# Two-layer transformer block on one core: projection copies on ScalarE, maxima ahead of layer 1, an earlier output load

## The chip, the cores and the metric

The kernel runs on one core of a Trainium2 chip. The metric is the device time in microseconds. A profile of one execution was taken besides; its times are in microseconds (us) unless a row says ns. Engines are named as in the profile: PE (TensorE matmul), PEld (its weight loads), DVE (VectorE), ACT (ScalarE), POOL (GpSimd) and SP (the queue that issues most DMAs).

## The reference

Two layers act on `x` of 4 x 512 x 320 (batch, tokens, channels); the context is 4 x 1601 x 192. There are 20 heads of 16 channels. Cut to what is computed, one layer is:

```python
h1 = _ln(x, n1_g, n1_b)
x = _attn(h1, h1, q1, k1, v1, o1_w, o1_b, heads) + x          # self-attention
h2 = _ln(x, n2_g, n2_b)
x = _attn(h2, context, q2, k2, v2, o2_w, o2_b, heads) + x     # cross-attention
h3 = _ln(x, n3_g, n3_b)
a, g = jnp.split(h3 @ ff_w1 + ff_b1, 2, axis=-1)              # 320 -> 2 x 1280
x = a * gelu(g) @ ff_w2 + ff_b2 + x                           # exact gelu, 1280 -> 320
```

and `_attn` projects q, k and v, takes softmax(q k^T / 4) v for each head, and multiplies the joined heads by `o_w`. All is float32.

## The kernel before

**Units.** The work of a layer is cut into 20 self-attention units, 20 cross-attention units and 4 feed-forward units, in this order. An attention unit is one batch element and one group of four heads; its keys (512, or 1601) are taken in chunks of 128. A feed-forward unit is one batch element. `u.i` is a unit's number in the whole order, `u.l` its layer, `u.kind` one of self, cross and ff.

**A chunk.** For each of four heads PE multiplies keys by queries into a PSUM bank `st` (128 keys x 512 queries; q and k are split into two parts for precision) and adds the negated row maximum through a product with ones (L1324). ACT raises each of the four to an exponential `pr` (L1334). PE then multiplies the chunk's `pr` with the values into one bank `av` (L1350); ACT copies that into `vo` (L1369), and POOL adds it to the unit's sum `o` (L1370). The values carry a column of ones, so the sum of the exponentials comes out beside them. The step from one `av` to the next is called a chunk below.

**What runs beside it.** The row maxima have to be known before a unit's scores: tiles `sps` of the scores of the unit ahead are made by PE (L1076, the last short key span L1101) and reduced by DVE (L1087, L1111) into `nmax` or `pm`. When all are there, L1155, L1158 and L1163 (`max_end`) negate, split and transpose them, and L1171 sends them by DMA to `nrows`. Between chunks PE also does the projections of later units: values `vps` (L1035), keys of the context `kps` (L972), queries `qps` (L947), queries and keys of self-attention `qkps` (L908), and the output projection `ops` (L1250).

**Copies out of PSUM.** The banks `vps` and `kps` are emptied by a copy that `taken` (L1011 to L1018) places: the recorded program keeps an estimate of when PE, DVE and ACT will be through with what they were given (`expect`), and the copy goes on DVE (L1014) where DVE's estimate is the earlier one, otherwise on ACT (L1017). `expect` also decides which of the eight PSUM banks a product gets: the one that comes free first. So a copy on another engine changes later choices of banks, and the places at which fillers are put.

**Order.** Everything is put in a fixed order when the program is recorded; the engines run their rows in that order. Small pieces of work sit in chains ("values", "proj", "divide" and others) with a due round, a round being one step of the record between groups of matmuls. After each chunk some are taken whose due rounds come and whose conditions hold. `giver` chooses, for a unit `u` that is running, the units ahead whose maxima tiles it may take beside its own work, and how many of them in each half chunk; for an attention unit these are the next two, for a feed-forward unit, before, the next one.

**Output.** When a batch element's heads are summed, `o` is written to memory (`oway`), read back in the layout of the output projection in three parts `aT` with the reciprocal sums `rT` (`load`, L1224 and L1225), POOL multiplies each part (`divide`, L1232), and PE projects (`project`, L1250). Each of these steps waits for a number of rounds after an earlier step: `since(i, n)` is n rounds after the i-th noted step. The third part's load follows its condition `since(4, 7)`, its multiply `since(5, 3)`, where the fifth note is made by that load.

**Feed-forward.** PE makes 320 to 2 x 1280 (L1435, L1495), ACT the gelu (L1506), DVE the product (L1507), PE the second product `yps` (L1542), and DVE adds it to `x` (L1549) for each of four blocks of 128 tokens.

Of the kernel before, what the change touches and what calls it, by code (L numbers as in the profile page):

```python
# [78 lines left out]
def kernel(ctx: ExitStack, tc: tile.TileContext, x, context, ws, out):  # L79
# [329 lines left out]
    expect = {"pe": 0.0, "act": 0.0, "dve": 0.0}  # L409
# [3 lines left out]
    def bank(name):  # L413
        i = min(range(NB), key=lambda i: bank_free[i])
        assert bank_free[i] < HELD, name
        t = psum.tile([P, 512], F32, tag=f"bank{i}", name=name)
        bank_of[id(t)] = [i, t, bank_free[i], 0.0]
        bank_free[i] = HELD
        return t
# [6 lines left out]
    def busy(engine, us, *tiles):  # L426
        expect[engine] = max([expect[engine]] + [bank_of[id(t)][3] + 0.05 for t in tiles]) + us
        for t in tiles:
            bank_free[bank_of[id(t)][0]] = expect[engine] + 0.09
# [12 lines left out]
    def add(chain, cost, f, due, ready=yes, soon=yes):  # L442
        chains[chain].append((cost if isinstance(cost, tuple) else (cost,), due, ready, soon, f))
# [566 lines left out]

    def taken(to, part, ps, us):  # L1011

        if expect["dve"] < expect["act"]:
            nc.vector.tensor_copy(to, part)  # L1014
            busy("dve", us, ps)
        else:
            nc.scalar.copy(to, part)  # L1017
            busy("act", us, ps)  # L1018
# [160 lines left out]
    def add_finish(u):  # L1179

        when = [clock["round"]]

        def since(i, n):
            return lambda: len(when) > i and clock["round"] >= when[i] + n

        def turn():

            way = o_way[u.b % 2]  # L1190
            dma(out=way[:, u.g * HG : (u.g + 1) * HG].rearrange("s j n -> j s n"), in_=u.o)
            if u.g == G - 1:
                held["written"] += 1
                errands.append((clock["round"] + 3, yes, sums))

        def sums():

            den = two.tile([P, N], F32, tag="rT", name="den")[:, : H * N // P]
            dma(out=den, in_=o_way[u.b % 2][DH].rearrange("h n -> (h n)").rearrange("(p c) -> p c", p=P))
            when.append(clock["round"])  # L1200

            def invert():
                nc.vector.reciprocal(den, den)
                busy("dve", 0.75)
                when.append(clock["round"])

            def save():
                dma(out=r_way[u.b % 2].rearrange("h n -> (h n)").rearrange("(p c) -> p c", p=P), in_=den)
                errands.append((clock["round"] + 3, lambda: held["open"] < 1, read))

            add("divide", LIGHT, invert, r - 20, yes, since(1, 3))
            add("divide", 0.0, save, r - 20, yes, since(2, 1))

        def read():

            held["read"] += 1
            held["open"] += 1
            aT = one.tile([P, 3, N], F32, tag="aT", name="aT")
            way, part = o_way[u.b % 2], {}

            def load(k, at, n):
                heads = slice(at // DH, (at + n) // DH)
                part[k] = two.tile([P, N], F32, tag="rT", name="rT")
                dma(out=aT[:n, k, :], in_=way[:DH, heads])  # L1224
                dma(  # L1225
                    out=part[k][:n],
                    in_=r_way[u.b % 2][heads].rearrange("(o j) n -> o j n", o=1).to_broadcast([DH, n // DH, N]),
                )
                when.append(clock["round"])

            def divide(k, n):
                nc.gpsimd.tensor_tensor(aT[:n, k, :], aT[:n, k, :], part[k][:n], ALU.mult)  # L1232

            for k, at, n in DK[:2]:
                load(k, at, n)
            first, second, third = DK
            add("divide", 0.0, lambda: divide(0, first[2]), r - 20, yes, since(4, 3))
            add("divide", 0.0, lambda: divide(1, second[2]), r - 20)
            add("divide", 0.0, lambda: load(*third), r - 20, yes, since(4, 7))
            add("divide", 0.0, lambda: divide(2, third[2]), r - 20, yes, since(5, 3))  # L1240
            add("divide", 0.0, lambda: end(aT), r - 20)

        def project(aT, t, part):
            cols = slice(part * D // 2, (part + 1) * D // 2)
            ps = bank("ops")
            written(0.93, ps)
            busy("dve", 0.3, ps)
            for k, at, n in DK:
                for f, m in tiles_of(P):
                    nc.tensor.matmul(  # L1250
                        ps[f : f + m, : D // 2],
                        lhsT=aT[:n, k, f * NQ + t * SLOT : f * NQ + t * SLOT + m],
                        rhs=wo[:n, k, cols],
                        start=(k == 0),
                        stop=(k == 2),
                    )
            nc.vector.tensor_tensor(xs[u.b][:, t, cols], ps[:, : D // 2], xs[u.b][:, t, cols], ALU.add)

        def end(aT):
            now = clock["round"]  # L1260
            for t in range(NQ):
                for part in range(2):
                    add(
                        "project", (0.317,) * 3, lambda t=t, part=part: project(aT, t, part),
                        now + 2 + u.nch * t + u.nch // 2 * part, yes, lambda: clock["round"] >= now + 1,
                    )
            add("project", 0.0, done, now + 2 + u.nch * NQ)

        def done():
            held["open"] -= 1  # L1270
            after(u)

        r = when[0]
        add("divide", 0.0, turn, r - 20, lambda: u.g or held["written"] < held["read"] + 2, since(0, 2))
# [327 lines left out]
    def left(v):  # L1602
        return sum(map(len, v.pairs))
# [19 lines left out]
    def giver(u):  # L1623

        ahead, coming = [], []
        for v in units[u.i + 1 : u.i + AHEAD + 1]:
            if v.kind == "ff":
                break  # L1630
            coming.append(v)
            if v.i <= u.i + 2 and (v.i == u.i + 1 or u.kind != "ff") or v.early:
                ahead.append(v)
                if v.pairs is None:
                    v.pairs = max_pairs(v)
        owed = 0.0
        last = clock["round"]

        def give(h, alone=False):
            nonlocal owed, last  # L1640
            rounds = []
            went = clock["round"] - last if alone else 1
            last = clock["round"]
            total = 0
            most = 0.0
            urgent = None
            for v in coming:
                if v not in ahead:
                    total += v.steps
                    continue  # L1650
                total += left(v)


                rest = v.start - (7 if alone else 4) - clock["round"]
                if rest > 0:
                    most = max(most, (total - rest * (not alone)) / (2 * rest))
                if left(v) and (rest == 1 or alone and rest < 1):
                    urgent = urgent or v
                    owed = max(owed, 1.0 if alone and rest > -4 else (left(v) + 1) // 2)
            owed += most * went if total else 0.0  # L1660
            while owed >= 1.0 and any(left(v) for v in ahead) and not (alone and rounds and rest > -4):
                hand = [v for v in ahead if left(v) and all(v.pairs) and at_hand(v)]
                if not hand and ahead[0].start - 4 - clock["round"] > 1:
                    break
                v = hand[0] if hand else next(v for v in ahead if left(v))
                if u.kind == "self" and ahead[-1].early and urgent is None:

                    v = ahead[-1]
                    if v not in hand:
                        break  # L1670
                at_once(v)
                rounds.append([f for q in v.pairs if q for f in q.popleft()[1]])
                owed -= 1.0
            owed = min(owed, 2.0)
            for v in ahead:
                mine = v.pairs[h % 2]
                if mine and not alone and at_hand(v):
                    return mine.popleft(), rounds
            return (False, []), rounds

        return give
# [46 lines left out]
    for i, u in enumerate(units):  # L1728
# [10 lines left out]
        for k in (3, SOON, AHEAD):  # L1739
            v = units[i + k] if i + k < len(units) else None  # L1740
# [32 lines left out]
```

## Time and profile before

| | |
|---|---|
| median of 3 runs | 2933.25 us (2932.35 to 2940.54) |
| profiled execution | 2933.88 us |
| its span, and mean granted clock | 2931.7 us, 0.994 |
| PE, DVE, ACT, POOL busy | 2863.0, 2069.9, 1881.4, 1299.4 us |
| copies of L1014 on DVE | 300 |
| copies of L1017 on ACT | 132 |

Layer 0's self-attention units run in about the first 290 us, its cross-attention units until about 1200, its feed-forward until 1505; layer 1 follows in the same order. In a row of the timeline the first number is the start from the span's beginning, the second the length of the row (a row may hold several instructions, xN), then engine, line, operation, output and inputs, and in brackets how long the engine was idle before it and what ended that. Busy shares of PE count a matmul that waits inside a run as busy, so PE's share does not tell how near it is to its limit; the length of chunks tells more.

### The profile page before, as it was taken

The numbers are of one execution on the slowest core, as the hardware profiler recorded it, in microseconds if no ns is written. First come the engines' busy times: TensorE is split into PE (matmuls) and PEld (weight loads), VectorE is DVE, ScalarE is ACT, GpSimd is POOL, SyncE is SP. The second block draws the span as 40 slices with busy tenths as digits, with TensorE's granted clock in tenths as the row PEclk, the third lists the DMA queues.
The fourth block names the chain that finished last, engine by engine and source line by source line (L and its number), as shares of the span: only waits on it lengthen the run. The fifth ranks groups of instructions, "written<-read, shape, count | busy, mean of one in ns | idle before, by whom it ended". The sixth has DMA issues, their size and how long they took to land.

```text
span 2931.7 us, 83446 instructions
## 1 busy us (share of the span) xinstructions
PE 2863.0 (98%) x35018; PEld 1540.3 (53%) x35018; DVE 2069.9 (71%) x4052; ACT 1881.4 (64%) x3733; POOL 1299.4 (44%) x1409
## 2 busy tenths in 40 slices
PE   8999999999999999999999999999999999999999
PEld 4445555555555555355554555555555555544554
DVE  6776888888888888323258678888888888872221
ACT  3767677887887888501138666778878778783000
POOL 3656345555545545211125663456455565551100
PEclk8999999999999999999999999999999999999999
DMA  3443223232232222200113342222221122222000
GB/s 106 113 120 99 68 73 101 59 85 62 49 93 61 54 54 62 84 17 11 42 38 88 99 104 69 58 62 53 62 65 47 50 72 51 53 56 76 22 20 14
DMA packets 163495, 188.59 MB, mean 64 GB/s; under 512 B 61988, under 2 KB 109104, under 8 KB 163120
## 3 DMA queue, kind: packets, MB, share of 16 engines
q1 hardware_dynamic: 162616, 181.69, 24.4%
q8 instruction: 275, 4.51, 0.6%
q10 hardware_dynamic: 472, 1.58, 0.2%
q14 instruction: 100, 0.82, 0.1%
q0 software_dynamic: 32, 0.00, 0.0%
HBM read 55.76 MB, written 29.36 MB: 29 GB/s over the span
## 4 chain that ended last, share of the span: by engine, by line
PE 87%; DVE 5%; POOL 2%; DMA 2%; ACT 2%; issue 1%; SPq 1%; ACTq 0%; POOLq 0%; DVEq 0%
PE av L1350 22%; PE st L1324 20%; PE fps L1435 10%; PE sps L1076 8%; PE yps L1542 6%; PE vps L1035 5%; PE kps L972 4%; PE ops L1250 4%; PE qkps L908 3%; PE fps L1495 3%; DVE nmax L1087 2%; PE qps L947 2%; DMA oway<-o 1%; PE sps L1101 1%; ACT pr L1334 1%
## 5 line engine op out<-in xcount | busy, mean ns | idle before, releaser
L1334 ACT ACTIVATE pr<-st 128x512 f32<-128x512 f32 (+1 forms) x2720 | 1404.5, 604 | 394.3 <-PE st L1324 359.3
L1087 DVE TENSOR_REDUCE pm<-sps 128x1 f32<-128x512 f32 (+1 forms) x1920 | 1147.8, 660 | 138.7 <-PE sps L1076 132.4
L1370 POOL TENSOR_TENSOR o<-o,vo 128x512 f32<-128x512 f32 x576 | 739.8, 1284 | 950.8 <-ACT vo L1369 942.0
L1076 PE MATMUL sps<-kT,q 32*128 32x512 f32 (+1 forms) x4800 | 869.0, 421 | 12.2 <-DMA q<-halves 4.4
L1324 PE MATMUL st<-q,kT 32*128 32x512 f32 (+1 forms) x5120 | 790.7, 420 | 2.8 <-ACT o L1364 2.4
L1350 PE MATMUL av<-pr,vals 128*32 128x512 f32 (+1 forms) x5440 | 734.5, 606 | 35.0 <-ACT pr L1334 13.4
L1324 PEld LDWEIGHTS st<-q,kT 32*128 32x128 f32 (+1 forms) x5120 | 448.5, 180 | 297.4 <-ACT pr L1334 117.5
L1324 PE MATMUL st<-nrows,ones 32*128 32x512 f32 (+1 forms) x2720 | 560.6, 399 | 4.8 <-DMA nrows<-turned 4.7
L1076 PEld LDWEIGHTS sps<-kT,q 32*128 32x128 f32 x4800 | 429.8, 184 | 73.7 <-DVE nmax L1087 14.6
L1087 DVE TENSOR_REDUCE nmax<-sps 128x1 f32<-128x512 f32 x640 | 396.7, 682 | 92.7 <-PE sps L1076 89.2
L1369 ACT COPY vo<-av 128x512 f32<-128x512 f32 x576 | 353.0, 613 | 17.4 <-PE av L1350 10.3
L1506 ACT ACTIVATE gl<-fps,b 128x512 f32<-128x512 f32 x80 | 54.7, 687 | 408.9 <-PE fps L1495 299.1
L1435 PE MATMUL fps<-hT,w 128*128 128x512 f32 x640 | 283.1, 597 | 0.0
L1350 PEld LDWEIGHTS av<-pr,vals 128*32 128x32 f32 (+1 forms) x5440 | 110.9, 108 | 309.9 <-DVE pm L1087 175.8
L1324 PEld LDWEIGHTS st<-nrows,ones 32*128 32x128 f32 (+1 forms) x2720 | 264.6, 180 | 14.8 <-DMA nrows<-turned 6.0
L1507 DVE SCALAR_TENSOR_TENSOR hid<-fps,b,gl 128x512 f32<-128x512 f32 x80 | 59.7, 748 | 242.6 <-ACT gl L1506 240.5
L1435 PEld LDWEIGHTS fps<-hT,w 128*128 128x128 f32 x640 | 119.2, 190 | 155.1 <-issue 152.2
L1542 PE MATMUL yps<-w,hid 128*128 128x320 f32 x640 | 175.5, 434 | 0.0
L1542 PEld LDWEIGHTS yps<-w,hid 128*128 128x128 f32 x640 | 120.6, 190 | 56.1 <-ACT gl L1506 5.3
L1250 PEld LDWEIGHTS ops<-wo,aT 112*32 112x32 f32 (+1 forms) x3072 | 99.3, 111 | 63.1 <-issue 29.5
L1250 PE MATMUL ops<-wo,aT 112*32 112x160 f32 (+1 forms) x3072 | 126.1, 302 | 5.5 <-POOL aT L1232 5.0
L527 POOL TENSOR_SCALAR root<-root 128x4 f32<-128x4 f32 x22 | 5.2, 234 | 266.8 <-DVE root L521 266.7
(91 smaller groups left out, 2544.1 us busy)
## 6 DMA issues: line engine op xcount, KB each, us to landing
kT<-stages SPq DMA_DIRECT2D x80, 400.5 KB
oway<-o SPq DMA_DIRECT2D x80, 256.0 KB
q<-halves SPq DMA_DIRECT2D x80, 256.0 KB
q<-halves SPq DMA_DIRECT2D x27, 512.0 KB
kT<-halves SPq DMA_DIRECT2D x40, 256.0 KB
aT<-oway SPq DMA_DIRECT2D x32, 224.0 KB
rT<-rway SPq DMA_DIRECT2D x32, 224.0 KB
hT<-hturned SPq DMA_DIRECT2D x96, 64.0 KB
```

The lines of the kernel that those rows point to most:

```text
L972: nc.tensor.matmul(ps[(i * GT + f) * SLOT : (i * GT + f + 1) * SLOT, :w], lhsT=wk2[:, k, u.g * GD + f * SLOT : u.g * GD + (f + 1) * SLOT], ...
L1035: nc.tensor.matmul(ps[f : f + m, :w], lhsT=u.kvT[:n, k, at + f : at + f + m], rhs=wv[:n, k, h0 * DH : h1 * DH], start=(k == 0), stop=(k == ...
L1076: nc.tensor.matmul(own[0][:, :w], lhsT=u.queries(slice(j * SLOT, (j + 1) * SLOT), e, t), rhs=u.kT[j * SLOT : (j + 1) * SLOT, u.k0 + at : u ...
L1087: nc.vector.tensor_reduce(to, own[0][:, :w], AX.X, ALU.max)
L1250: nc.tensor.matmul(ps[f : f + m, : D // 2], lhsT=aT[:n, k, f * NQ + t * SLOT : f * NQ + t * SLOT + m], rhs=wo[:n, k, cols], start=(k == 0) ...
L1324: nc.tensor.matmul(own[0][:r, :], lhsT=ones[rows, :r] if e == 2 else u.keys(rows, c), rhs=u.rows[rows, :] if e == 2 else u.queries(rows, e ...
L1334: nc.scalar.activation(p[:r], own[0][:r], AF.Exp)
L1350: nc.tensor.matmul(ps[j * SLOT : (j + 1) * SLOT, :], lhsT=columns_of[:r, head : head + SLOT], rhs=pr.pop((c, j))[:r, :], start=True, stop= ...
L1369: nc.scalar.copy(vo, ps)
L1370: nc.gpsimd.tensor_tensor(u.o, u.o, vo, ALU.add)
L1435: nc.tensor.matmul(ps, lhsT=w1[:, k, i * FF + c * P : i * FF + (c + 1) * P], rhs=natural(u.hT[:, k]), start=start, stop=stop,)
L1542: nc.tensor.matmul(ps[:, :D], lhsT=hid[c][:, t * P : (t + 1) * P], rhs=w2[:, c, :], start=(c == 0), stop=(c == NHC - 1),)
```

## The change

1. `taken` no longer compares: all copies of `vps` and `kps` are made by ACT (L1017).
2. `giver` lets a feed-forward unit take the maxima of the next two units as well. Only layer 0's last feed-forward has attention units right behind it, so this is the one place.
3. In layer 1 the third output load asks for five rounds after its mark, not seven.

```diff
     def taken(to, part, ps, us):
 
-        if expect["dve"] < expect["act"]:
+        if False:
             nc.vector.tensor_copy(to, part)
             busy("dve", us, ps)
         else:
...
-            add("divide", 0.0, lambda: load(*third), r - 20, yes, since(4, 7))
+            add("divide", 0.0, lambda: load(*third), r - 20, yes, since(4, 5 if u.l else 7))
             add("divide", 0.0, lambda: divide(2, third[2]), r - 20, yes, since(5, 3))
...
-            if v.i <= u.i + 2 and (v.i == u.i + 1 or u.kind != "ff") or v.early:
+            if v.i <= u.i + 2 or v.early:
                 ahead.append(v)
```

**DVE at the end of layer 0's last feed-forward.** `x_110` is the residual stream, `nmax_95` holds the maxima of layer 1's first unit and later those of its third, `nmax_96` those of the second. Before:

```order
L1549 TENSOR_TENSOR x_110<-yps,x_110 128x320
L1155 TENSOR_REDUCE nmax_95<-nmax_95 128x4x4
L1158 TENSOR_REDUCE nmax_95<-nmax_95 128x4x4
L1163 STREAM_TRANSPOSE turned<-nmax_95 128x32
L1549 TENSOR_TENSOR x_110<-yps,x_110 128x320
L1087 TENSOR_REDUCE nmax_96<-sps 128x1 x16
L1087 TENSOR_REDUCE nmax_95<-sps 128x1 x8
L1155 TENSOR_REDUCE nmax_96<-nmax_96 128x4x4
```

With the change:

```order
L1549 TENSOR_TENSOR x_110<-yps,x_110 128x320
L1087 TENSOR_REDUCE nmax_96<-sps 128x1 x4
L1155 TENSOR_REDUCE nmax_95<-nmax_95 128x4x4
L1158 TENSOR_REDUCE nmax_95<-nmax_95 128x4x4
L1163 STREAM_TRANSPOSE turned<-nmax_95 128x32
L1549 TENSOR_TENSOR x_110<-yps,x_110 128x320
L1087 TENSOR_REDUCE nmax_96<-sps 128x1 x12
L1087 TENSOR_REDUCE nmax_95<-sps 128x1 x4
L1155 TENSOR_REDUCE nmax_96<-nmax_96 128x4x4
```

Four reduces of the second unit went ahead of the first unit's `max_end`; between the last addition to `x` and the second unit's `max_end` there are 16 reduces, before 24.

**POOL in layer 1's self-attention,** at the output of the second batch element. Before:

```order
L1370 TENSOR_TENSOR o<-o,vo 128x512
L625 TENSOR_SCALAR hturned<-x_110,mv,root_25977 128x4x32
L625 TENSOR_SCALAR hturned<-x_110,mv,root_25977 128x3x32 x2
L827 CAST halves<-halves 128x512
L828 TENSOR_TENSOR halves<-halves 128x512
L1370 TENSOR_TENSOR o<-o,vo 128x512
L1232 TENSOR_TENSOR aT<-aT,rT 96x512
```

With the change:

```order
L1370 TENSOR_TENSOR o<-o,vo 128x512
L1232 TENSOR_TENSOR aT<-aT,rT 96x512
L625 TENSOR_SCALAR hturned<-x_110,mv,root_25961 128x4x32
L625 TENSOR_SCALAR hturned<-x_110,mv,root_25961 128x3x32 x2
L827 CAST halves<-halves 128x512
L828 TENSOR_TENSOR halves<-halves 128x512
L1370 TENSOR_TENSOR o<-o,vo 128x512
```

The third multiply went ahead of the layer norm's `hturned`, of the split of `halves` and of one addition to `o`.

**DVE in layer 0's cross-attention,** a stretch with copies, a piece of layer norm (L521 to L525, L561, L562) and the context's transposes (L757). Before:

```order
L1087 TENSOR_REDUCE pm<-sps 128x1 x4
L1014 COPY vals<-vps 128x12x16
L561 BN_STATS st_16441<-x_110 128x6
L562 BN_AGGR mv<-st_16441 128x2
L1087 TENSOR_REDUCE pm<-sps 128x1 x4
L1014 COPY stages<-kps 128x200
L757 STREAM_TRANSPOSE stages<-stages 128x6x32 x2
L521 TENSOR_SCALAR root_16507<-mv 128x4
L522 TENSOR_SCALAR root_16510<-root_16507 128x4
```

With the change:

```order
L1087 TENSOR_REDUCE pm<-sps 128x1 x4
L561 BN_STATS st_16441<-x_110 128x6
L562 BN_AGGR mv<-st_16441 128x2
L1087 TENSOR_REDUCE pm<-sps 128x1 x4
L757 STREAM_TRANSPOSE stages<-stages 128x6x32 x2
L521 TENSOR_SCALAR root_16507<-mv 128x4
L522 TENSOR_SCALAR root_16510<-root_16507 128x4
```

The two copies left DVE's order; the rest stands as it was.

## The prediction

> **What bounds the kernel now.** I read the page first, then the waits, then the timeline of the chunks. The page gives the busy time of each engine.
>
> ```profile
> PE 2863.0 (98%) x35018; PEld 1540.3 (53%) x35018; DVE 2069.9 (71%) x4052; ACT 1881.4 (64%) x3733; POOL 1299.4 (44%) x1409
> ```
>
> PE is almost never idle by this count, but a matmul that waits inside a run of others still counts as busy, so I look at what its weight loads (PEld) and matmuls wait for. The waits view has total us, times, longest.
>
> ```profile
> PEld av L1350 <- DVE pm L1087: 175.8, 392, 1.5
> ...
> ACT stages L1017 <- PE kps L972: 10.1, 16, 1.0
> ...
> PE ops L1250 <- POOL aT L1232: 5.0, 2, 3.6
> ```
>
> The long row is not lost time of that size: it says that the `av` product at the end of a chunk stands behind a maximum of DVE, while score matmuls drain. A chunk is 128 keys of one unit, from one `av` to the next, and how long it takes is the measure of this kernel. The timeline of the matmuls of L1350 (start, length) gives it.
>
> ```profile
> 781.99 1.06 PE L1350 MATMUL av<-pr,vals 128*32 128x512 f32 x8
> 784.47 1.07 PE L1350 MATMUL av<-pr,vals 128*32 128x512 f32 x8
> 787.61 1.07 PE L1350 MATMUL av<-pr,vals 128*32 128x512 f32 x8
> 790.41 1.06 PE L1350 MATMUL av<-pr,vals 128*32 128x512 f32 x8
> ```
>
> These steps are 2.48, 3.14 and 2.80 us. The first and the last chunk hold no copy, the middle one does. So 0.32 us of difference exists where no copy is, and a copy costs mostly because its projection takes PE time.
>
> **Edit 1, all copies on ScalarE.** The groups of the two copy lines say how much moves (min/median/max ns, first and last start; then the two kinds of wait of PE for it):
>
> ```profile
> L1014 DVE COPY vals<-vps x177: 277/293/360, 66.4 to 2589.7; 128x128 f32<-128x128 f32 x85, 128x192 f32<-128x192 f32 x78, 65x192 f32<-65x192 f32 x8, 65x128 f32<-65x128 f32 x6
> L1014 DVE COPY stages<-kps x123: 366/367/370, 213.6 to 2542.5; 128x200 f32<-128x200 f32 x92, 128x201 f32<-128x201 f32 x31
> ...
>   PEld sps L1076: 2.4, 2
>   PEld st L1324: 2.1, 7
>   PE sps L1076: 1.6, 1
> ```
>
> and for ACT:
>
> ```profile
> L1017 ACT COPY vals<-vps x95: 262/318/381, 34.9 to 2586.6; 128x192 f32<-128x192 f32 x50, 128x128 f32<-128x128 f32 x43, 65x128 f32<-65x128 f32 x2
> L1017 ACT COPY stages<-kps x37: 326/327/387, 214.3 to 2555.8; 128x200 f32<-128x200 f32 x28, 128x201 f32<-128x201 f32 x9
> ...
>   PEld sps L1076: 2.2, 3
>   PEld st L1324: 1.7, 7
>   PE sps L1076: 1.4, 1
> ```
>
> 300 copies move: DVE loses 177 x 0.293 + 123 x 0.367 = 97.0 us, ACT gains 177 x 0.318 + 123 x 0.327 = 96.5. Then DVE stands at 1973 us and ACT at 1978: neither is over-full as a sum, and 132 of 432 copies already go the new way. The question is what a chunk gains. Most often nothing, as these neighbours show:
>
> ```profile
> 826.83 1.06 PE L1350 MATMUL av<-pr,vals 128*32 128x512 f32 x8
> 828.49 0.27 ACT L1017 COPY vals<-vps 128x128 f32<-128x128 f32 x1
> 829.72 1.07 PE L1350 MATMUL av<-pr,vals 128*32 128x512 f32 x8
> 831.31 0.28 DVE L1014 COPY vals<-vps 128x128 f32<-128x128 f32 x1
> 832.62 1.06 PE L1350 MATMUL av<-pr,vals 128*32 128x512 f32 x8
> ```
>
> 2.89 us with the copy on ACT, 2.90 with it on DVE: the copy hides behind the score matmuls on either engine. Where DVE is late with its maxima it does not hide:
>
> ```profile
> 2501.00 1.06 PE L1350 MATMUL av<-pr,vals 128*32 128x512 f32 x8
> 2502.87 0.37 DVE L1014 COPY stages<-kps 128x201 f32<-128x201 f32 x1
> 2504.33 1.06 PE L1350 MATMUL av<-pr,vals 128*32 128x512 f32 x8 [0.21 <-ACT pr L1334]
> ...
> 2507.41 1.06 PE L1350 MATMUL av<-pr,vals 128*32 128x512 f32 x8
> ```
>
> 3.33 us with the DVE copy, 3.08 in the chunk behind it, whose copy of the same size is on ACT. Counting chunk lengths against chunks with the same projections, I find 28 of this kind with an excess near 0.18 (the first starts at 319.34, this is the last): 28 x 0.18 = 5.0 us. Four more are late by 0.75 to 1.07, because transposes or layer norm work stand on DVE there too; this is the first:
>
> ```profile
> 895.86 1.06 PE L1350 MATMUL av<-pr,vals 65*32 65x512 f32 x8 [0.22 <-ACT pr L1334]
> ...
> 897.74 0.37 DVE L1014 COPY stages<-kps 128x200 f32<-128x200 f32 x1
> ...
> 900.72 1.06 PE L1350 MATMUL av<-pr,vals 128*32 128x512 f32 x8 [1.10 <-DVE pm L1087]
> ```
>
> Of each the copy is at most 0.37: 4 x 0.37 = 1.5, with the others 6.5. Against it, the waits for copies change hands. PE's matmul waits are 1.6 for L1014 and 1.4 for L1017, which is 3.2 over 300 copies instead of 132: +1.6. The weight loads' waits, part of which lies under matmuls still running, are 4.5 and 3.9, or 8.9 over 300: +4.4. I take the middle, 3.0: 3.0 - 6.5 = **-3.5**. The bounds: the late chunks and the waits for L1014 all go and nothing comes back, -6.5 - 4.5 = -11.0; or no late chunk gains, +4.4.
>
> **Edit 2, maxima in layer 0's last feed-forward.** Before layer 1's first chunks can run, DVE reduces the maxima of the coming units. One group of eight matmuls (four tiles) now enters the feed-forward, and eight reduces in all leave the stretch behind it.
>
> ```profile
> 1493.33 0.74 PE L1076 MATMUL sps<-kT,q 32*128 32x512 f32 x8
> ...
> 1505.75 14.44 DVE L1087 TENSOR_REDUCE nmax<-sps 128x1 f32<-128x512 f32 x24 [0.18 <-PE sps L1076]
> ...
> 1520.94 1.94 PE L1350 MATMUL av<-pr,vals 128*32 128x512 f32 x8
> ```
>
> DVE is busy without a gap for 24 reduces, 14.44 / 24 = 0.602 each, and the second unit's row maxima stand behind all of them. With 16 it has 8 x 0.602 = 4.8 less to do. The feed-forward grows by one group on PE, 0.74, as such a group took inside it at 1493.33; its four reduces fit into DVE's idle time there. Unit 0's last maximum now stands behind four reduces, 2.4 us later; as DVE still has work for 16 x 0.602 = 9.6 us before unit 1's row is there, this is covered, and costs up to 2.4 if it is not. Sum 0.74 - 4.8: **-4.1 (bounds -4.8 and 0.74 + 2.4 = +3.1)**.
>
> **Edit 3, third load two rounds sooner in layer 1.** The load releases POOL's third multiply, for which PE waited once in layer 1.
>
> ```profile
> 1642.86 1.29 POOL L1370 TENSOR_TENSOR o<-o,vo 128x512 f32<-128x512 f32 x1
> ...
> 1649.38 1.26 POOL L1232 TENSOR_TENSOR aT<-aT,rT 96x512 f32<-96x512 f32 x1
> ...
> 1650.69 2.12 PE L1250 MATMUL ops<-wo,aT 96*32 96x160 f32 x56 [3.60 <-POOL aT L1232]
> ```
>
> In the changed order the multiply follows the first row directly, so it would run from about 1644.15 to 1645.4 instead of 1649.38 to 1650.6. PE reaches the product today at 1650.69 - 3.60 = 1647.09, and one chunk (2.9) sooner in the changed order, 1644.2. It would wait 1645.4 - 1644.2 = 1.2 instead of 3.60: **-2.4**. The bounds: the whole wait goes, -3.6; or the hturned work that now stands behind the multiply is 1.26 late for the next projection, with the wait as it was, +1.3. The loads also pass the queue of SP: at five places two issues move ahead of the row maxima's transfer.
>
> ```profile
> 1500.75 2.65 SPq L1171 DMA_DIRECT2D nrows<-turned  x4
> ```
>
> 2.65 / 4 = 0.66 an issue, 5 x 2 x 0.66 = 6.6 us if every one held PE up. The row is fetched for the unit ahead, with chunks of the present one still to run; I take nothing for it and keep 6.6 as a rival.
>
> **Sum.** The profiled execution took 2933.88 us (its span of 2931.7 and 2.2 around it), 0.6 above the median of 2933.25. 2933.9 - 3.5 - 4.1 - 2.4 = 2923.9; less the 0.6, **2923**.
>
> **Rivals.** *Banks and not copies* (0.22): the late chunks wait for a free PSUM bank or for the draining scores; 2.80 against 2.48 without any copy speaks for it, 3.33 against 3.08 against it. Edit 1 is then worth nothing: 2933.25 - 6.5 = 2927. [...]
>
> *ScalarE becomes the bound* (0.08), the slower side. Copies stand in ACT's queue ahead of the next chunk's exponentials:
>
> ```profile
> 897.13 0.62 ACT L1369 COPY vo<-av 128x512 f32<-128x512 f32 x1
> ...
> 899.17 2.06 ACT L1334 ACTIVATE pr<-st 128x512 f32<-128x512 f32 x4 [0.53 <-PE st L1324]
> ```
>
> A chunk of 128-wide values asks ACT for 2.06 + 0.62 + 0.32 = 3.00 us where chunks take 2.90: 0.10 x 91 such copies = 9.1. A key copy waits for its product, 10.1 us over the 37 of today or 0.27 each, so 3.01 + 0.27 = 3.28 against 3.14; if every second one is not made good, 0.14 x 123 / 2 = 8.6. With edits 2 and 3 at -6.5 that is +11.2: 2944.5. It decides once the exponentials follow each other without the 0.53 of idle time seen here; that idle time, and 2.89 with an ACT copy at 828.49, speak against it.
>
> *Row maxima late on SP* (0.08): the forecast plus 6.6, 2930. For it speaks that five places change alike; against it, that the rows have chunks of lead.
>
> *More than the sum* (0.12): edit 1 reaches -11.0 and edit 3 -3.6, and the clock stays up behind the feed-forward. Today it falls (PE, PEld, DVE, ACT, POOL busy, granted clock, DMA share, GB/s):
>
> ```profile
> 1516.00:1518.00 2.00, 2.00 (x10) 1.00 (x7) 2.00 (x5) 0.00 (x0) 0.00 (x0) 0.50 0.00 0
> ```
>
> The `av` at 1520.94 takes 1.94 us at this clock, 1.06 elsewhere, a loss of 0.9. Sum -11.0 - 4.1 - 3.6 - 0.9 = -19.6: 2914. [...]
>
> *An edit that does not do what it says* (0.05): the number of maxima is the same over the kernel, and if the second unit's rest is simply taken from elsewhere, edit 2 gives nothing; 2927.
>
> **How the numbers follow.** The forecast has 0.45. What this kernel's measurement can tell is about 0.3%, 8.8 us: faster means below 2924.5, slower above 2942. The forecast is just on the faster side, so I give it 0.33 faster and 0.12 same. More than the sum adds 0.12 to faster; banks, SP and the void edit hold 0.35, of it 0.03 faster (sums near the edge), 0.30 same and 0.02 slower (edit 1 at its upper bound); ScalarE adds 0.02 to same and 0.06 to slower. Together 0.48, 0.44, 0.08. The range goes from 2912, a little below the largest sum, to 2938, which is edit 1 at +4.4 with edits 2 and 3 at nothing (2937.7); only the ScalarE case lies wholly outside.
>
> **What would show it.** Right: the 28 late chunks lose about 0.18 each and the step from 2501.00 reads near 3.1; behind the feed-forward one run of 16 reduces of 0.60 us; the wait of 3.60 for aT near 1.2. Wrong: ACT exponentials with no idle time before them and narrow chunks at 3.0; `av` waiting for pr more than for pm in sum without shorter chunks; waits of scores for nrows; the hole behind the feed-forward as long as before.

## The result and the profile after

| | time, us | runs | mean granted clock of the profiled execution |
|---|---|---|---|
| before | 2934.56 (2928.87 to 2940.54) | 22 | 0.994 |
| changed | 2928.36 (2925.80 to 2932.57) | 22 | 0.994 |

The ratio is 0.9981, interval 0.9975 to 0.9987: 5.6 us less (0.0019 x 2934.56), between 3.8 and 7.3. That is a gain, but a smaller one than the 0.3% that the prediction set as its bound for "faster". The forecast of 2923, 10 less than before, had the sign right and nearly twice the size; the range of 2912 to 2938 holds the time.

The page of the changed kernel shows that the copies went where they should:

```profile
PE 2863.1 (98%) x35018; PEld 1545.3 (53%) x35018; DVE 1980.7 (68%) x3752; ACT 1950.1 (67%) x4033; POOL 1299.5 (44%) x1409
```

DVE lost 300 instructions and 89 us, ACT gained 300 and 69. PE did the same work. The waits of the changed kernel, in the form shown before (total us, times, longest):

```profile
PEld av L1350 <- DVE pm L1087: 186.7, 414, 2.4
...
PE st L1324 <- DMA nrows<-turned: 7.0, 8, 1.6
...
PE ops L1250 <- POOL aT L1232: 3.8, 3, 2.1
```

The waits of PE for `aT` went from 5.0 in 2 to 3.8 in 3. The longest of before, 3.60 in layer 1, is 1.38 now; the 2.1 stands in layer 0's self-attention, which edit 3 leaves alone. The waits of scores for `nrows` rose; before, this row reads:

```profile
PE st L1324 <- DMA nrows<-turned: 4.7, 5, 2.3
```

To see where time goes I use the 680 copies out of `av` (L1364, L1366, L1369), which stand in the same order in every kernel here, and compare when each of them starts. The change in lead over a stretch is what the stretch gained. Worked out so, in us, against the profiled execution of before (negative is sooner):

| kernel (edits) | layer 0's attention (copies 0 to 320) | feed-forward and first units of layer 1 (320 to 360) | rest of layer 1's self-attention (360 to 400) | layer 1's cross-attention (400 to 679) |
|---|---|---|---|---|
| changed (1, 2, 3) | -1.2 | -3.7 | -4.1 | +4.0 |
| 1 | +0.5 | 0.0 | +4.7 | -2.1 |
| 2 | +0.3 | -5.6 | -0.5 | +1.6 |
| 3 | +2.7 | +1.1 | -4.2 | +3.6 |
| 2, 3 | +0.7 | -5.6 | -4.3 | +4.7 |
| 3 in cross-attention only | +0.6 | -0.4 | -0.4 | +10.1 |
| 1, 2, 3 in self-attention only | -3.5 | -2.9 | -4.2 | +0.7 |
| 1, 2 | -0.4 | -4.3 | -0.1 | +0.2 |
| 1, 2, 3, rows issued first | +5.9 | -4.7 | -4.2 | +1.5 |
| 2, 3 in self-attention only | +2.1 | -5.6 | -4.2 | +1.1 |

These are single executions. The kernels without edit 1 are equal in layer 0's attention, and differ there by up to 2.7; the five with edit 1 are equal there too, and lie between -3.5 and +5.9. So the first column tells little, and a cell of the others may be off by some us as well: edit 1's +4.7 goes with the clock, which was at half there for 13.7 us, before for 3.4 (mean clock of the whole execution 0.992 and 0.994). The last two columns still tell the main story. Edit 3 takes 4.1 to 4.3 off layer 1's self-attention wherever it is applied there. In layer 1's cross-attention it costs 3.6 to 10.1 wherever it is applied with the order on SP that comes with it, where the kernels without it lie between -2.1 and +1.6.

**The granted clock.** Much of the table's scatter may be this. In the profiled execution of before PE's clock stands at 0.50 in five stretches of 3.4 to 13.7 us, each a multiple of 3.4; in the changed kernel's there are six of the same kind, and not all in the same places. The mean clock of the 14 profiled executions is 0.991 to 0.996. Over all 218 timed runs of this study (each with its own mean granted clock, one level for each kernel), a run is 1.84 us longer for each 0.001 of mean clock that it is lower, and 0.60 of the variance of the times goes with the clock. "At an equal clock" below means after taking that off. It is a way to see through the scatter and no fair price: part of an edit's own cost may stand in the clock. In the run of the load sooner in the cross-attention only, the clock fell within 2 us of the end of a wait of 1.53 us (below); that the wait brought it down is not shown.

### The profile page after: what moved, and what is told of

Same layout as the page of the kernel before. It is cut to its first block, busy times and chain, and to the rows that moved or that the text cites. A ratio compares the mean times of both kernels' runs of the same rounds, so it can differ in the third digit from the quotient of the medians.

```text
span 2927.9 us, 83288 instructions
## 1 busy us (share of the span) xinstructions
PE 2863.1 (98%) x35018; PEld 1545.3 (53%) x35018; DVE 1980.7 (68%) x3752; ACT 1950.1 (67%) x4033; POOL 1299.5 (44%) x1409
## 4 chain that ended last, share of the span: by engine, by line
PE 85%; DVE 6%; POOL 4%; issue 2%; DMA 2%; ACT 1%; SPq 1%; POOLq 0%; ACTq 0%; DVEq 0%
PE av L1350 21%; PE st L1324 19%; PE fps L1435 10%; PE sps L1076 8%; PE yps L1542 6%; PE vps L1035 5%; PE ops L1250 3%; PE kps L972 3%; PE qkps L908 3%; PE fps L1495 3%; DVE nmax L1087 2%; DVE pm L1087 2%; PE qps L947 2%; POOL o L1370 1%; PE sps L1101 1%
## 5 line engine op out<-in xcount | busy, mean ns | idle before, releaser
L1076 PE MATMUL sps<-kT,q 32*128 32x450 f32 (+1 forms) x4800 | 870.7, 422 | 10.7 <-DMA q<-halves 4.3
L1369 ACT COPY vo<-av 128x512 f32<-128x512 f32 x576 | 352.9, 613 | 15.2 <-PE av L1350 8.5
L1111 DVE TENSOR_REDUCE pm<-sps 128x4 f32<-128x508 f32 x160 | 98.9, 681 | 36.1 <-PE sps L1101 33.0
```

The source lines that it names most:

```text
L1076: nc.tensor.matmul(own[0][:, :w], lhsT=u.queries(slice(j * SLOT, (j + 1) * SLOT), e, t), rhs=u.kT[j * SLOT : (j + 1) * SLOT, u.k0 + at : u ...
L1111: nc.vector.tensor_reduce(u.pm[:, :, j, ns - 1], ps[:, : NQ * w].rearrange("p (t w) -> p t w", w=w)[:, :, :n], AX.X, ALU.max,)
L1369: nc.scalar.copy(vo, ps)
```

## The experiments

**The edits one at a time.** Edit 1 alone:

```diff
-        if expect["dve"] < expect["act"]:
+        if False:
             nc.vector.tensor_copy(to, part)
```

> Edit 1 alone: all copies on ScalarE, edits 2 and 3 left as before. In the trace of the changed kernel layer 0's cross-attention runs as long as before (the copy out of the last chunk of it starts 0.2 us sooner), while layer 1's cross-attention loses 4 us, the last chunk being 4.0 sooner where it had been 8.7 sooner. Theory SP (the loss in layer 1's cross-attention comes from edit 3, whose loads stand ahead of the row maxima): copies are worth nothing, -1 to +1 us. Theory ACT (the loss comes from ScalarE with its copies): about +4 us. The prediction's step: -3.5 us.

Measured: 0.999 of the time before (0.998 to 1.0), 2.9 us less; at an equal clock 4.8 +- 1.3 less. The interval of the times just reaches no gain; by the equal clock edit 1 does bring something, near the predicted 3.5. Theory ACT is out: layer 1's cross-attention did not lose in this profile, it gained 2.1. Theory SP had the place of the loss, but not the worth of the copies.

Edit 2 alone:

```diff
-            if v.i <= u.i + 2 and (v.i == u.i + 1 or u.kind != "ff") or v.early:
+            if v.i <= u.i + 2 or v.early:
```

> Edit 2 alone: the last feed-forward of layer 0 takes maxima of two units. Both theories: -3.6 us, as the changed kernel's trace shows between the end of layer 0's cross-attention and chunk 360 (from 0.2 sooner to 3.85 sooner). The prediction's step was -4.1; its upper bound +3.1 holds if the later row maximum of the first unit is not covered.

Measured: 0.9992 (0.9983 to 1.0), 2.3 us less. In the profile the stretch around the feed-forward gained 5.6. At an equal clock the kernel gains 0.3 +- 1.4: its mean clock over the runs was 0.9948 against 0.9933 before, so what it brings comes along with the clock. That is read more closely below.

Edit 3 alone:

```diff
-            add("divide", 0.0, lambda: load(*third), r - 20, yes, since(4, 7))
+            add("divide", 0.0, lambda: load(*third), r - 20, yes, since(4, 5 if u.l else 7))
```

> Edit 3 alone: the third output load two rounds sooner in layer 1. Theory SP: about -4 us in layer 1's self-attention and +4 to +5 in its cross-attention, where PE waits for nrows at three places, so -1 to +1 in all. Theory ACT: -4 us, since the cross-attention keeps its time. The prediction's step: -2.4.

Measured: 1.0004 (0.9992 to 1.0016), no gain. The table shows why: -4.2 in the self-attention, +3.6 in the cross-attention.

Edits 2 and 3 without edit 1:

```diff
-        if False:
+        if expect["dve"] < expect["act"]:
             nc.vector.tensor_copy(to, part)
```

> Edit 1 undone, edits 2 and 3 kept: where the comparison of the two estimates decides the copy's engine again. Theory SP: as the changed kernel, 0.9980 +- 0.0005 of the time before. Theory ACT: 4 us less than the changed kernel, 0.9967 of the time before. The prediction's step: 3.5 us more than the changed kernel, 0.9993.

Measured: 0.9987 (0.9978 to 0.9996). The changed kernel's 0.9981 lies within this, so these two alone do not settle edit 1; but layer 1's cross-attention loses 4.7 with the old copies as well, which takes ScalarE out as the cause of that loss.

**What edit 3 costs in the cross-attention.** The timeline of the changed kernel at the last of three like places (SPq rows are issues on SP's queue):

```profile
2495.74 0.21 DVE L1163 STREAM_TRANSPOSE turned<-nmax 128x32 f32<-128x32 f32 x1
...
2496.80 2.56 POOL L1232 TENSOR_TENSOR aT<-aT,rT 112x512 f32<-112x512 f32 x2
...
2498.13 0.54 SPq L1225 DMA_DIRECT2D rT<-rway  x1
...
2498.78 2.66 SPq L1171 DMA_DIRECT2D nrows<-turned  x4
...
2499.35 1.07 PE L1350 MATMUL av<-pr,vals 128*32 128x512 f32 x8
...
2502.64 0.50 PE L1324 MATMUL st<-nrows,ones 32*128 32x512 f32 x2 [0.87 <-DMA nrows<-turned]
...
2503.54 1.06 PE L1350 MATMUL av<-pr,vals 65*32 65x512 f32 x8
```

The row maxima are turned and ready at 2495.95. Their four issues stand on SP behind the third load of `rT`, and they start when it has left the queue; the first score of the next unit waits for them, and the chunk takes 4.19 us. The load itself is late because it waits for POOL: it is to fill the buffer of `rT` (there are two) that the first of the two multiplies from 2496.80 still reads. So the rows stand for 2.83 us behind a load that cannot go yet, and not for the time of two issues; it is 2.83 at all three places. SP's waits show it (total us, times, longest):

```profile
SPq L1225 <- POOL aT L1232: 63.4, 11, 12.5
```

In the kernel before they are 10.5 in 5, the longest 3.4, and the same place there reads:

```profile
2504.10 2.65 SPq L1171 DMA_DIRECT2D nrows<-turned  x4
...
2506.80 0.60 SPq L1224 DMA_DIRECT2D aT<-oway  x1
...
2507.41 1.06 PE L1350 MATMUL av<-pr,vals 128*32 128x512 f32 x8
2507.51 0.60 SPq L1225 DMA_DIRECT2D rT<-rway  x1
...
2510.17 1.07 PE L1350 MATMUL av<-pr,vals 65*32 65x512 f32 x8
```

Here the rows go first, 3.31 us before that `av` and not 0.57, and the chunk takes 2.76. Two runs test whether this is the cause: the load sooner in the cross-attention only, and sooner everywhere but there.

```diff
-            add("divide", 0.0, lambda: load(*third), r - 20, yes, since(4, 7))
+            add("divide", 0.0, lambda: load(*third), r - 20, yes, since(4, 5 if u.l and u.cross else 7))
```

> The third output load two rounds sooner in layer 1's cross-attention alone, nothing else changed. In the trace of edit 3 alone three chunks there wait for nrows, whose transfer stands behind the two loads on SP, and around each of them 1.2 to 1.8 us are lost, 4.9 together. Theory SP: +4 to +5 us, with waits of scores for nrows up to 1.9 us. Rival (the loads themselves do no harm, the loss came from fillers that shifted because of layer 1's self-attention): 0 +- 1 us.

Measured: 1.0029 (1.0018 to 1.0041), 8.5 us more; at an equal clock 5.2 +- 1.7 more. The difference between the two is the clock, as its timeline and windows (PE, PEld, DVE, ACT, POOL busy, granted clock, DMA share, GB/s) at the second of the three places show:

```profile
2302.37 2.67 SPq L1171 DMA_DIRECT2D nrows<-turned  x4
2303.07 1.07 PE L1350 MATMUL av<-pr,vals 128*32 128x512 f32 x8
2307.01 0.49 PE L1324 MATMUL st<-nrows,ones 32*128 32x512 f32 x2 [1.53 <-DMA nrows<-turned]
2307.90 1.23 PE L1350 MATMUL av<-pr,vals 65*32 65x512 f32 x8
...
2312.52 1.07 PE L1350 MATMUL av<-pr,vals 128*32 128x512 f32 x8
```

```profile
2306.00:2308.00 2.00, 0.99 (x16) 0.65 (x20) 0.75 (x2) 0.49 (x1) 0.47 (x1) 1.00 0.05 8
2308.00:2310.00 2.00, 2.00 (x24) 0.83 (x24) 1.29 (x2) 2.00 (x5) 0.00 (x0) 0.67 0.00 0
2310.00:2312.00 2.00, 2.00 (x24) 1.56 (x20) 0.70 (x2) 0.06 (x1) 1.86 (x2) 0.50 0.00 0
2312.00:2314.00 2.00, 2.00 (x39) 1.01 (x36) 2.00 (x4) 1.93 (x5) 0.65 (x1) 0.98 0.18 15
```

After the wait (PE busy 0.99 of 2.00) the clock is at half for some 3.4 us, so two chunks are long at this place: 4.83 us from 2303.07 to 2307.90 and 4.62 to 2312.52, where the kernel before has 2.76 and 3.13.

```diff
-            add("divide", 0.0, lambda: load(*third), r - 20, yes, since(4, 5 if u.l else 7))
+            add("divide", 0.0, lambda: load(*third), r - 20, yes, since(4, 5 if u.l and not u.cross else 7))
```

> Edits 1 and 2 as they are, edit 3 in layer 1's self-attention alone. Theory SP: 4 to 5 us less than the changed kernel, 0.9965 of the time before, and no more than five waits of scores for nrows. Rival (loads harmless): as the changed kernel, 0.998.

Measured: 0.9962 (0.9949 to 0.9974), 2922.3 us against 2933.87 in the same comparison, on 5 runs. This is the fastest kernel of the study, about 11 us faster than before and by the ratios about 5.6 faster than the changed one (0.9981 - 0.9962). At the same place its rows go first again and the chunk (2496.15 to 2498.91) takes 2.76:

```profile
2492.53 2.65 SPq L1171 DMA_DIRECT2D nrows<-turned  x4
...
2495.22 0.60 SPq L1224 DMA_DIRECT2D aT<-oway  x1
...
2496.15 1.07 PE L1350 MATMUL av<-pr,vals 128*32 128x512 f32 x8
...
2498.91 1.06 PE L1350 MATMUL av<-pr,vals 65*32 65x512 f32 x8
```

Is it the order on the queue, or something else that the earlier load brings along? The next run keeps all three edits and puts only the rows ahead:

```diff
-        if u.cross and u.before.cross:
+        if u.cross and u.before.cross and not u.l:
             u.rows_of = rows
             errands.appendleft((clock["round"] + 1, yes, rows))
         else:
             rows()
```

> The changed kernel (all three edits), but in layer 1 the row maxima's transfer is issued as soon as it may be, not one round later. On SP this puts the four nrows issues between cross-attention units ahead of the third loads again; the loads stay where edit 3 put them. Theory SP order (the harm of edit 3 in the cross-attention is that nrows stands behind two loads in the queue): 5 to 8 us less than the changed kernel, 0.996 of the time before, as the run that left the cross-attention out of edit 3 (0.9962). Rival (the loads' own traffic, or POOL's earlier multiply, does the harm): as the changed kernel, 0.998.

Measured: 0.9974 (0.9965 to 0.9984). It lies between the two theories (0.996 and 0.998), and the time alone does not part it from the changed kernel. In its profile layer 1's cross-attention loses 1.5 where the changed kernel lost 4.0, and the chunk at that place is 3.13 in place of 4.19. So by the profile, one execution, the order on SP is the larger part of the harm. The rest of the distance to 0.9962 is in other stretches of single executions, and within the intervals; I do not claim a cause for it.

Edit 3 undone altogether (edits 1 and 2):

```diff
-            add("divide", 0.0, lambda: load(*third), r - 20, yes, since(4, 5 if u.l else 7))
+            add("divide", 0.0, lambda: load(*third), r - 20, yes, since(4, 7))
```

> Edit 3 undone, edits 1 and 2 kept. By the runs of single edits at an equal granted clock (edit 1 -4.8, edit 2 -0.2, edit 3 +1.7), 1.7 less than the changed kernel; by the prediction's step for edit 3, 2.4 more. The granted clock: if edit 2 spares the dip behind the feed-forward, none is seen there near 1515.

Measured: 0.9974 (0.996 to 0.9987). The changed kernel is 0.9981: edit 3 as made gave nothing back, more likely took 2 us.

**What edit 1 brings, and by what.** All copies on ScalarE change two things: the engine that makes them, and, by the planner's estimates, the PSUM bank that each later product gets. The order of instructions on PE, POOL and SP is the same with and without edit 1 when nothing else is changed: the estimates choose the copies' engine and the banks, not, as the description of the kernel has it, the places of fillers. Two runs take the two apart. The engine only:

```diff
         if expect["dve"] < expect["act"]:
-            nc.vector.tensor_copy(to, part)
+            nc.scalar.copy(to, part)
             busy("dve", us, ps)
```

> All copies on ScalarE, but the planner counts them as before, on DVE where its estimate was earlier, so that every other instruction keeps its place. Theory copies (the late chunks wait for DVE's copy): -3 to -6 us at an equal granted clock, as edit 1 alone shows there (-4.8), and the step from 2501.00 near 3.1 instead of 3.33. Rival banks (what edit 1 brings comes from the other order of fillers and banks): 0 +- 1.5 us at an equal clock.

Measured: 1.0002 (0.9993 to 1.0012); at an equal clock -1.4 +- 1.5. The banks only (each copy stays on its engine of before, from a list of the 432 choices):

```diff
+    ENGINES = (
...
+    )
...
-        if expect["dve"] < expect["act"]:
+        engine = ENGINES[start.setdefault("copies", 0)]
+        start["copies"] += 1
+        if engine == "D":
             nc.vector.tensor_copy(to, part)
-            busy("dve", us, ps)
         else:
             nc.scalar.copy(to, part)
-            busy("act", us, ps)
+        busy("act", us, ps)
```

> Each of the 432 copies stays on the engine that it had before, but the planner counts them all on ScalarE, as in edit 1 alone; only the PSUM banks that products get are then other than before. Theory banks: what edit 1 brings, about -3 to -5 us at an equal granted clock (edit 1 alone -4.8, copies moved with old banks -1.4), comes from here: -3 us or more. Rival (engine and banks bring it only together): 0 +- 1.5.

Measured: 1.0018 (1.0009 to 1.0027), 5.3 us more. So by the times neither half brings the gain: the engine alone nothing that can be told from the noise, the banks alone a loss, both together 2.9 less. One chunk shows it, the one at 2501.00 on which the prediction rested. With edit 1 alone (both):

```profile
2502.16 1.06 PE L1350 MATMUL av<-pr,vals 128*32 128x512 f32 x8
...
2504.09 0.38 ACT L1017 COPY stages<-kps 128x201 f32<-128x201 f32 x1
2505.29 1.06 PE L1350 MATMUL av<-pr,vals 128*32 128x512 f32 x8
...
2508.37 1.07 PE L1350 MATMUL av<-pr,vals 128*32 128x512 f32 x8
```

3.13 and then 3.08. With the engine only (the copy keeps its line number L1014, but is on ACT):

```profile
2504.86 1.06 PE L1350 MATMUL av<-pr,vals 128*32 128x512 f32 x8
...
2506.79 0.39 ACT L1014 COPY stages<-kps 128x201 f32<-128x201 f32 x1
2508.18 1.07 PE L1350 MATMUL av<-pr,vals 128*32 128x512 f32 x8 [0.21 <-ACT pr L1334]
```

3.32, as the 3.33 before, and `av` waits 0.21 for ACT as before. With the banks only (its lines are numbered ten higher):

```profile
2504.90 1.06 PE L1360 MATMUL av<-pr,vals 128*32 128x512 f32 x8
2506.77 0.37 DVE L1025 COPY stages<-kps 128x201 f32<-128x201 f32 x1
2508.50 1.07 PE L1360 MATMUL av<-pr,vals 128*32 128x512 f32 x8 [0.48 <-DVE pm L1097]
```

3.60, with a wait for a maximum of DVE that has grown to 0.48. What the 0.21 waits for can be read from the order in the kernel before:

```profile
2500.53 2.06 ACT L1334 ACTIVATE pr<-st 128x512 f32<-128x512 f32 x4 [0.55 <-PE st L1324]
...
2503.68 2.06 ACT L1334 ACTIVATE pr<-st 128x512 f32<-128x512 f32 x4 [0.60 <-PE st L1324]
```

The `av` at 2504.33 multiplies the first four exponentials, which are through at 2502.59; the second four are those of the next chunk. It starts when the first of the second four is through, at 2504.28. So it does not wait for data. What an exponential frees besides is the PSUM bank of its scores, and the wait for a maximum of DVE can be read in the same way. That `av` had been given this bank is a reading and not shown: the trace does not show banks.

The other chunks agree with this one. Against the same steps before, 28 steps with a DVE copy are 0.17 to 0.19 shorter in the profile of edit 1 alone, 5.1 us together. With the engine only, 27 of these 28 are as long as before. So this gain is there only when the engine and the planner's account change together. Not all late chunks are of this kind: the steps from 2136.82 and 2345.64 in the kernel before, 4.86 and 4.85 long as the one from 895.86 in the prediction (4.86), are 1.07 shorter with edit 1, and as much with the engine only.

The mirror of the engine run, all copies on DVE with the banks of before:

```diff
         else:
-            nc.scalar.copy(to, part)
+            nc.vector.tensor_copy(to, part)
             busy("act", us, ps)
```

> The mirror of the run that moved all copies to ScalarE with the banks of before: here the 132 copies of ScalarE go to DVE, the banks as before. Theory engine does not matter: 0 +- 2 us at an equal clock. The prediction's step (a DVE copy makes a late chunk 0.18 later): some of 132 chunks more are late, +2 to +6 us, or more where DVE copies follow each other.

Measured: 1.0051 (1.0039 to 1.0064), 15 us more; at an equal clock 11.9 +- 2.0. So the engine does matter in this direction: 15 / 132 = 0.11 us for each copy that DVE takes on. Whether DVE had no room for them is not shown by this alone, as here too the planner counts copies on another engine than the one that makes them. That 300 such copies cost nothing in the run of the engine only speaks for DVE's load; a run in which the planner counts all copies on DVE was not made.

Last, edit 2 and the harmless part of edit 3, without edit 1:

```diff
-        if False:
+        if expect["dve"] < expect["act"]:
             nc.vector.tensor_copy(to, part)
...
-            add("divide", 0.0, lambda: load(*third), r - 20, yes, since(4, 5 if u.l else 7))
+            add("divide", 0.0, lambda: load(*third), r - 20, yes, since(4, 5 if u.l and not u.cross else 7))
```

> Edit 2, and edit 3 in layer 1's self-attention alone; the copies as before. Against the same kernel with edit 1 (0.9962) it tells what edit 1 is worth where the loads do no harm. By the sums at an equal granted clock edit 1 brings about 5 us: 0.9978 of the time before. If what edit 1 seemed to bring was chance of the clock: 0.996.

Measured: 0.9984 (0.9975 to 0.9994). With edit 1 the same kernel is 0.9962, so here edit 1 is worth 0.0022 x 2932 = 6.4. In the four places where it can be compared it is worth 2.9 (alone), 5.3 (beside edit 2: 0.9992 to 0.9974), 1.8 (beside 2 and 3: 0.9987 to 0.9981) and 6.4: 4.1 in the mean, each with an uncertainty of about 3.

## Why the prediction was right or wrong

**Edit 1, -3.5: right in size, with half of its reason.** The mean of four comparisons is -4.1. 28 steps did gain about 0.18 each, 5.1 us against the 28 x 0.18 = 5.0 counted, though they are not all the counted ones (the first starts at 70.65), and the step from 2501.00 is 3.14 in the changed kernel. But the step "3.33 us with the DVE copy, 3.08 in the chunk behind it" read the copy's engine as the cause, and the run of the engine alone left that chunk at 3.32. The rival "banks and not copies" had half of the cause, and said that edit 1 would then be worth nothing; the planner's estimates that it changes set the banks as well, which neither the forecast nor the rival reckoned with. ScalarE did not become the bound; with 1950.1 us it is busy for 67% of the span.

**Edit 2, -4.1: near in size, its cause not told apart from the clock.** With it the stretch from the end of layer 0's attention to copy 360 gained 2.9 to 5.6 in seven profiles; without it it moved by -0.4 to +1.1 in the three others of the table. In the run of edit 2 alone DVE's rows are as worked out, 16 reduces in 9.83 us, with the first unit's maxima behind four reduces and no wait for them:

```profile
1502.92 2.48 DVE L1087 TENSOR_REDUCE nmax<-sps 128x1 f32<-128x512 f32 x4 [0.17 <-PE sps L1076]
...
1509.16 9.83 DVE L1087 TENSOR_REDUCE nmax<-sps 128x1 f32<-128x512 f32 x16 [0.16 <-PE sps L1076]
```

In the changed kernel's profiled execution the same stretch is cut up: the clock stands at 0.50 from 1509.9 to 1516.7, and DVE waits for PE:

```profile
1506.34 6.07 DVE L1087 TENSOR_REDUCE nmax<-sps 128x1 f32<-128x512 f32 x10 [0.16 <-PE sps L1076]
1512.64 1.29 DVE L1087 TENSOR_REDUCE nmax<-sps 128x1 f32<-128x512 f32 x2 [0.23 <-PE st L1324]
1515.62 2.48 DVE L1087 TENSOR_REDUCE nmax<-sps 128x1 f32<-128x512 f32 x4 [1.69 <-PE sps L1076]
```

```profile
1510.00:1512.00 2.00, 1.92 (x17) 1.60 (x17) 2.00 (x5) 0.64 (x2) 0.00 (x0) 0.50 0.28 64
```

That the clock "stays up behind the feed-forward", which the prediction kept for its larger rival, came true in the three profiles with edit 2 and without edit 1, and in none of the four with both. By the timings edit 2 alone is worth 2.3 with an interval from 0 to 5. The clock is in the stretch's gain: before, it was at half there for 10.2 us, 5.1 us of clock lost, and in the three profiles with 5.6 not at all. The kernel with edit 3 in the self-attention only was at half there for 10.2 us too and gained 2.9. So DVE's row is 4.6 shorter, 14.44 to 9.83, but how much of the 5.6 this gives by itself is not shown.

**Edit 3, -2.4: its gain was larger, and the cost that decides was set to nothing.** The self-attention gained 4.1 to 4.3. The wait of 3.60 that the sum was made on became 1.38, against the 1.2 worked out:

```profile
1640.24 1.26 POOL L1232 TENSOR_TENSOR aT<-aT,rT 96x512 f32<-96x512 f32 x1
...
1641.55 0.48 PE L1250 MATMUL ops<-wo,aT 96*32 96x160 f32 x8 [1.38 <-POOL aT L1232]
```

So the wait gave 2.2 of the 2.4 worked out. The rest goes with the clock: in this stretch it fell to half before (at 1744) and with the engine only, edits 1 and 2, the banks only and all copies on DVE (at 1644 to 1659), all without edit 3 here, and not in the changed kernel, with the rows first, or in the two with edit 3 in the self-attention only; one piece of 3.4 us at half is 1.7 us of clock lost.

The step that failed is "I take nothing for it": the two issues that pass the row maxima on SP. The prediction priced them at 6.6 if they held PE up at all five places and gave the case 0.08, because "the rows have chunks of lead". They have not: before, the maxima are turned at 2504.03 and the first score reads them at 2508.98, less than two chunks later. The issues start 3.31 us ahead of the last full `av`, and that suffices. The price was of the wrong thing as well: not the 0.66 of an issue held the rows, but the load's own wait for POOL, 2.83 us at each of three places. The run of the cross-attention alone lost 8.5, and that of edit 3 alone gained nothing. This is the missing half of the forecast: -3.5 - 4.1 - 2.4 = -10.0 was expected, and the kernel with edit 3 in the self-attention only measured about -11.

So the gain came out at about half since one term, written down as a rival, belonged into the sum. That rival's 2930 has the right mechanism with a price of the wrong thing. That the banks rival's 2927 is close to 2928.4 is chance: it reached it by a loss of edit 1's gain, and the loss is edit 3's.

## What to carry to other kernels

When a step is issued sooner, look at every transfer that it passes on the same queue, and ask how far ahead of its reader that transfer now starts. Ask too what the step itself still has to wait for there, such as its own buffer, since here the row maxima behind it on the queue waited as well, 2.83 us at each of three places. A lead of "chunks" has to be read off the timeline at the very place, not taken from the plan. An edit to a planner's rule changes all that the planner derives from it (here PSUM banks besides the engine), so an experiment has to move the two apart before one of them is called the cause. Split an edit by the stages that it touches: here one half was worth 4 us and the other cost as much.

## What the runs showed of the hardware

The granted clock in the traces of before and of the changed kernel stands at 1.00 or at 0.50, and each piece at 0.50 within the span lasts 3.4 us or a multiple of it. From 10 us of clock (6 pieces of 1.7, edits 2 and 3 in the self-attention only) to 27 (16 pieces, the engine only) were lost in an execution, 18.8 before; 10.2 of that fell in the first 50 us, and 11.9 in the changed kernel. Where it falls is not the same from one profiled execution to the next, one for each kernel: edit 2's stretch ran at 1.00 in three profiles and at 0.50 for 1.7 to 5.1 us of lost clock in the four that have edit 1 as well. What makes it fall at one place and not at another is not shown. Over 218 runs 0.001 of mean clock went with 1.84 us and 0.60 of the variance, so differences of a few us between executions of one kernel are in good part differences in these pieces.

At one place the fall goes with the copies: near 344 us, in layer 0's cross-attention, the clock fell in the changed kernel, with the engine only, with edits 1 and 2 and with the rows first, all with all copies on ScalarE, and not before, with the banks only, with all copies on DVE or with edits 2 and 3 in the self-attention only. There the score waits for the row maxima, 0.39 us before and 1.57 in the changed kernel (before first, then the changed kernel's row and its window):

```profile
344.59 0.50 PE L1324 MATMUL st<-nrows,ones 32*128 32x512 f32 x2 [0.39 <-DMA nrows<-turned]
```

```profile
343.55 0.50 PE L1324 MATMUL st<-nrows,ones 32*128 32x512 f32 x2 [1.57 <-DMA nrows<-turned]
```

```profile
346.00:348.00 2.00, 2.00 (x24) 1.01 (x20) 0.61 (x2) 0.92 (x2) 0.48 (x1) 0.50 0.04 13
```

The two chunks there take 2.8 us more together (5.06 and 4.57 before, 6.23 and 6.24 after). The rows' issues start no later against the chunk than before, and why the transfer lands later with the copies on ScalarE stays open.
